# Deformable gather over 32 tiles of two image rows in place of 33 tiles of padded positions, with a table whose borders are zeroed once

## The chip, the cores and the metric

The kernel runs on one core of a Trainium2 chip. A core has a matrix engine (TensorE, PE in the profile, with PEld for its weight loads), a vector engine (VectorE, DVE), a scalar engine (ScalarE, ACT), a general engine (GpSimd, POOL) and a sync engine (SyncE, SP) that only issues transfers here. Data lie in SBUF, a memory of 128 partitions; matrix products accumulate in PSUM; DRAM holds inputs, outputs and scratch tables, and 16 DMA engines move data in and out. The metric is the device time in microseconds of one execution: 6844.52 us before the change, the median of three runs that lie between 6835.98 and 6856.77.

## What is computed

Four layers in sequence act on four images of 192 channels and 64 by 64 positions, all in float32. The change touches the first layer only, and of that the deformable convolution, which feeds a channel attention:

```python
def deform_conv(x, w_p, b_p, w_d):
    off = conv2d(x, w_p, stride=1, pad=1) + b_p      # 18 offsets a position
    xp = jnp.pad(x, ((0, 0), (0, 0), (1, 1), (1, 1)))
    Hp, Wp = (H + 2, W + 2)                          # 66 x 66
    ...
    px = off[:, :N] + p0x + pn[0]                    # N = 9 taps
    py = off[:, N:] + p0y + pn[1]
    ...
    xo = g_lt * gat(qlx, qly) + g_rb * gat(qrx, qry) \
       + g_lb * gat(qlx, qry) + g_rt * gat(qrx, qly)
    ...
    return conv2d(xo, w_d, stride=KS, pad=0)

xn = layer_norm(x)
q = deform_conv(xn, w_p, b_p, w_d)
k_spe, v_spe = qkv(xn)
attn = softmax(q @ l2norm(k_spe).T * temperature)
```

Every output position and each of its nine taps needs a blend of four neighbouring pixels, at places that are known only at run time. The products of `q` with `k_spe` are sums over positions, so the kernel never forms `q`: it sums the outer products of the blended pixels with the normed pixels over all positions, for every tap, and applies the weights afterwards.

## The kernel before, in words

**Geometry.** An image normed by the first layer is held in SBUF as `xn`, 2 halves of 96 channels on partitions, by 66 x 66 positions with a border of zeros (`WP` = 66). `MID` = 67 is the place of the first real pixel. The kernel cuts the stretch from `MID` on into `NT` = 33 tiles of 128 successive padded positions. Some positions of each tile are border columns, with pixels of zero, so that they add zero to the sums.

**The table.** For each image a table in DRAM has one row for each padded position, with four quarters of 192 floats: the pixel and its right, lower and lower-right neighbours (3072 bytes a row). One gathered row is all that one tap of one position needs. There are two tables, used in turn by image; they are zeroed at the head and tail once, when the kernel begins (lines 317 to 327).

**`offsets(b)`, line 404**, has four stages. Eight steps of layer norm load an eighth of the image each (`xi`, line 431) and write it into `xn`. `write_table` (line 455) turns each tile of 128 positions by two transposes on PE (line 462), copies it from PSUM into a buffer `tt` by ACT (line 463), and after a group of G tiles stores the buffer four times, once for each quarter, shifted by the neighbour's place (line 466): G is 11, so 3 groups and 12 stores, or 3 where it is woven between other work, so 11 groups and 44 stores. Then `xn` itself is stored for later (line 471). `convolve` (line 473) computes the 18 offsets of each position by matmuls of 96 x 32 weights and 384 columns (three tiles; line 482); four such column groups make a batch, so that 33 tiles are 11 groups in batches of 4, 4 and 3. The result is turned (line 490) and added to the base positions `p0` (line 494), an input of 128 x 33 x 18 floats that is loaded for every image. Eight operations on DVE (lines 503 to 515) make the row indices `idx` and the blend weights.

**`gather(b)`, line 518**, goes through the nine taps in five groups, `[(0, 1), (2, 3), (4, 5), (6, 7), (8,)]`, and in each over the 33 tiles. One tile of a group loads its own pixels from the table's last quarter (line 566, 96 KB; for the last group straight into half of `xo`), gathers the rows of each tap by an indirect transfer that POOL issues (line 572) into a ring of 11 buffers, blends them by two operations on ACT and two on DVE (lines 578 to 583), and multiplies: three matmuls of 128 x 128 by 192 columns (line 590), each of which is two PE instructions in float32. The buffers of the tile (`xo`, `ti`, `row`) are threefold.

**Order.** For image 0, `gather` runs alone from about 115 us to 624 us of the trace ("stage A"), with its pixels kept in SBUF (`kept`, 33 tiles), and `offsets(1)` is woven in between: one step of it every few steps of the gather. For images 1 to 3 the gather is woven into the non-local attention of layer 1 of the image before. That layer goes through 16 query chunks of 256 positions (scores at line 920, exponential at line 984, product with the values at line 986), and `GATHER_STEPS` = 33 x 9 + 12 tells the weaver over how many steps to spread the gather. For images 2 and 3, the layer-norm steps of `offsets` alternate with the key projection of layer 1 (line 865 on), and the rest of `offsets` runs right after it, before the first query chunk is loaded (`xc`, line 909) and its first matmul (`th`, line 912). I call these stretches, which end near 2515 us and 4135 us, the transitions.

SP issues all plain transfers in program order into one queue. In a transition that order is: table stores, store of `xn`, two loads of `xc`, three loads of `ti`, two more of `xc`, then weights.

Of the kernel before, what the change touches and what calls it, by code (L numbers as in the profile page):

```python
# [10 lines left out]
F32 = mybir.dt.float32  # L11
# [9 lines left out]
P = 96  # L21
# [21 lines left out]

TROWS = 35 * 128
RING = 11
GATHER_STEPS = NT * 9 + 12
TAPS = [(0, 1), (2, 3), (4, 5), (6, 7), (8,)]


# [30 lines left out]
def conv_seq_kernel(ctx: ExitStack, tc: tile.TileContext, a, out: bass.AP):  # L80
# [236 lines left out]
    with pool_of(name="zero", bufs=1) as zp:  # L317
        zero = zp.tile([128, 4 * C], F32, tag="zero", name="zero")
        nc.gpsimd.memset(zero, 0.0)
        for i in range(2):  # L320
            t = dram.tile([TROWS, 4 * C], F32, tag=f"table{i}", name=f"table{i}")
            first, last = 2 * WP + 2, WP + 1 + NT * 128
            nc.sync.dma_start(out=t[0:128], in_=zero)
            nc.sync.dma_start(out=t[128:first], in_=zero[: first - 128])
            nc.sync.dma_start(out=t[last : last + 128], in_=zero)
            nc.sync.dma_start(out=t[last + 128 : TROWS], in_=zero[: TROWS - last - 128])
            tables.append(t)

    xn_flat = [dram.tile([C, XNW], F32, tag=f"xnd{i}", name=f"xnd{i}") for i in range(2)]
# [75 lines left out]
    def offsets(b, pool, kept=None, woven=False):  # L405
# [3 lines left out]
        table = tables[b % len(tables)]  # L409


        pos = pool.tile([128, NT, 18], F32, name=f"pos_{b}", tag="pos")
        fr = pool.tile([128, NT, 18], F32, name=f"fr_{b}", tag="fr")
        idx = pool.tile([128, NT, 9], I32, name=f"idx_{b}", tag="idx")
        xn = big.tile([P, 2, XNW], F32, tag="x", name=f"xn_{b}")
        xnv = xn[:, :, 0 : WP * WP].rearrange("p k (r c) -> p k r c", r=WP)
        for k in range(2):
# [7 lines left out]
        with ExitStack() as s:  # L425
            sb = s.enter_context(pool_of(name="l0a", bufs=1 if woven else 2))
            s1 = s.enter_context(pool_of(name="l0a1", bufs=1))
            ps = s.enter_context(pool_of(name="l0aps", bufs=2, space=PSUM))
            for i in range(NCH):
                xi = sb.tile([P, 2, CN], F32, tag="xi", name=f"xi_{b}_{i}", bufs=2)  # L430
                nc.sync.dma_start(out=xi, in_=given(b)[:, :, bass.ts(i, CN)])
                layer_norm(
                    xi, CN, xnv[:, :, 1 + 8 * i : 9 + 8 * i, 1:65], sb, ps, f"l0_{b}_{i}",
                    affine=(V["l0_g1"], V["l0_b1"]), rows=8,
                )
                yield

            wp = s1.tile([P, 2, 9, 32], F32, tag="wp", name=f"wp_{b}")
            given_wp = s1.tile([P, 2, 9, 18], F32, tag="given_wp", name=f"given_wp_{b}")
            nc.sync.dma_start(out=given_wp, in_=a["wp"].rearrange("(k p) t o -> p k t o", p=P))  # L440
            nc.gpsimd.memset(wp, 0.0)
            nc.gpsimd.tensor_copy(wp[:, :, :, 0:18], given_wp)
            bp = s1.tile([128, 1], F32, tag="bp", name=f"bp_{b}")
            nc.gpsimd.memset(bp, 0.0)
            for q in range(4):
                nc.sync.dma_start(out=bp[32 * q : 32 * q + 18, :], in_=a["bp"])
            p0 = s1.tile([128, NT, 18], F32, tag="p0", name=f"p0_{b}")
            nc.sync.dma_start(out=p0, in_=a["p0"])

            G, T = 3 if woven else 11, 3  # L450

            def write_table():
                for g in range(NT // G):
                    if kept is None:
                        tt = sb.tile([128, G, C], F32, tag="tt", name=f"tt_{b}_{g}", bufs=3 if woven else 2)
                    else:
                        tt = kept[:, bass.ts(g, G)]
                    for j in range(G):
                        t0 = (g * G + j) * 128 + MID
                        pt = ps.tile([128, C], F32, tag="tr", name=f"pt_{b}_{g}_{j}")  # L460
                        for k in range(2):
                            nc.tensor.transpose(pt[:, bass.ts(k, P)], xn[:, k, t0 : t0 + 128], ident[:P, :P])
                        nc.scalar.copy(tt[:, j, :], pt)
                    for q in range(4):
                        e = g * G * 128 + (2 - q // 2) * WP + 2 - q % 2
                        nc.sync.dma_start(
                            out=table[e : e + G * 128, bass.ts(q, C)].rearrange("(j p) c -> p j c", p=128), in_=tt
                        )
                    if not woven or g % 3 == 2:
                        yield  # L470
                nc.sync.dma_start(out=xn_drams[b % 2], in_=xn)

            def convolve():
                for g0 in range(0, NT // T, 4):
                    ng = min(4, NT // T - g0)
                    m = 32 * ng
                    po = ps.tile([128, T * 128], F32, tag="off", name=f"po_{b}_{g0}", bufs=1)
                    for tap in range(9):
                        for k in range(2):
                            for q in range(ng):  # L480
                                o = (g0 + q) * T * 128 + (tap // 3) * WP + tap % 3
                                nc.tensor.matmul(  # L482
                                    po[32 * q : 32 * q + 32], lhsT=wp[:, k, tap, :], rhs=xn[:, k, o : o + T * 128],
                                    start=tap == 0 and k == 0, stop=tap == 8 and k == 1,
                                )
                    ot = sb.tile([128, T * 128], F32, tag="ot", name=f"ot_{b}_{g0}")
                    nc.scalar.activation(ot[:m], po[:m], AF.Identity, bias=bp[:m])
                    pp = ps.tile([128, T, 4, 32], F32, tag="tr", name=f"pp_{b}_{g0}")
                    for j in range(T):
                        nc.tensor.transpose(  # L490
                            pp[:, j, 0:ng, :].rearrange("p q o -> p (q o)"), ot[:m, bass.ts(j, 128)], ident[:m, :m]
                        )
                    tiles = slice(g0 * T, (g0 + ng) * T)
                    nc.vector.tensor_tensor(
                        pos[:, tiles, :].rearrange("p (q j) o -> p j q o", j=T), pp[:, :, 0:ng, 0:18],
                        p0[:, tiles, :].rearrange("p (q j) o -> p j q o", j=T), ALU.add,
                    )
                    yield

            for part in (convolve(), write_table()) if woven else (write_table(), convolve()):  # L500
                yield from part

            nc.vector.tensor_scalar(pos, pos, -1.0, 65.0, ALU.max, ALU.min)
            fi = s1.tile([128, NT, 18], I32, name=f"fi_{b}", tag="fi")
            fl = s1.tile([128, NT, 18], F32, name=f"fl_{b}", tag="fl")
            nc.vector.tensor_copy(fi, pos)
            nc.vector.tensor_copy(fl, fi)
            nc.vector.tensor_tensor(fr, fl, pos, ALU.is_gt)
            nc.vector.tensor_tensor(fl, fl, fr, ALU.subtract)
            nc.vector.tensor_tensor(fr, pos, fl, ALU.subtract)  # L510
            nc.vector.tensor_scalar(pos, fr, -1.0, 1.0, ALU.mult, ALU.add)
            nc.vector.scalar_tensor_tensor(
                fl[:, :, 0:9], fl[:, :, 0:9], float(WP), fl[:, :, 9:18], ALU.mult, ALU.add
            )
            nc.vector.tensor_scalar(idx, fl[:, :, 0:9], float(MID), None, ALU.add)
        return pos, fr, idx

    def gather(b, s, at, m2, kept=None):
# [16 lines left out]
        for taps in TAPS:  # L535
# [16 lines left out]
                nc.sync.dma_start(out=wd[64:128, 1:12:3, :], in_=a["wd"][0:64, 1:9:2, :])  # L552
                nc.sync.dma_start(out=wd[:, 2:12:3, :], in_=a["wd"][64:C, 1:9:2, :])
            acc = [ps.tile([128, 512], F32, tag=f"h{h}", name=f"h{h}_{b}_{taps[0]}") for h in range(2)]
            for t in range(NT):

                e = t * 128 + MID
                xo = sb.tile([128, 2, C], F32, tag="xo", name=f"xo_{b}_{t}_{taps[0]}")
                if kept is not None:
                    tt = kept[:, t]  # L560
# [2 lines left out]
                else:  # L563
                    tt = xo[:, 1, :]
                if kept is None:
                    nc.sync.dma_start(out=tt, in_=table[e : e + 128, 3 * C : 4 * C])
                elif len(taps) == 1:
                    nc.gpsimd.tensor_copy(xo[:, 1, :], tt)
                for j, tap in enumerate(taps):
# [18 lines left out]
                for m in range(3):  # L588

                    nc.tensor.matmul(  # L590
                        acc[m // 2][:, bass.ts(m % 2, C)], lhsT=xo.rearrange("p j c -> p (j c)")[:, bass.ts(m, 128)],
                        rhs=tt, start=t == 0 and m % 2 == 0, stop=t == NT - 1, skip_group_check=True,
                    )
                yield
            m = 3 * (taps[0] // 2)
# [1262 lines left out]
    with ExitStack() as s:  # L1858
        sb = s.enter_context(pool_of(name="l0first", bufs=1))
        m2 = stats.tile([M, C + 3 * M], F32, tag="m2", name="m2_0")  # L1860
        kept = sb.tile([128, NT, C], F32, tag="kept", name="kept")
        at = links(offsets(0, sb, kept))
        beside = [constants(), offsets(1, second, woven=True)]
        for k, _ in enumerate(gather(0, s, at, m2, kept)):
# [132 lines left out]
```

## Time and profile before

| what | value |
|---|---|
| median of three runs | 6844.52 us (6835.98 to 6856.77) |
| profiled execution, first to last instruction | 6951.6 us |
| its mean granted PE clock | 0.938 |
| PE busy | 6255.4 us (90%), 45188 instructions |
| DVE busy | 4817.8 us (69%) |
| ACT busy | 3725.4 us (54%) |
| POOL busy | 2061.6 us (30%) |
| DMA | 743.45 MB, mean 107 GB/s |
| gathers, line 572 | 1188 (4 images x 9 taps x 33 tiles) |
| matmul instructions of the gather, line 590 | 2376 + 990 + 594 |
| transposes, line 462 | 264 |
| offset convolution, line 482 | 1584 instructions |

The profiled execution took 107 us more than the median run, so a number from the trace is 1.6% larger than the same work in the runs that give the time. The page's busy times say how long an engine had an instruction in hand, not that it worked at its peak; a time on an engine costs something only where nothing else is later. In a table of windows, each row gives a stretch from the start of the span in microseconds, its length, the busy time of each engine with the instructions in brackets, the granted PE clock as a share of full speed, the mean busy share of the 16 DMA engines, and what they moved.

### The profile page before, as it was taken

How to read it: one execution, taken by the hardware profiler on the slowest of the kernel's cores; microseconds unless marked ns; L12 is line 12 of the kernel's file. 1: busy time of each engine (PE TensorE's matmuls, PEld its weight loads, DVE VectorE, ACT ScalarE, POOL GpSimd, SP SyncE). 2: the span in 40 equal slices, each digit the busy share in tenths (PEclk: the TensorE clock that was granted, in tenths of full speed). 3: DMA queues.
4: the chain of work that ended last, by engine and by line, in shares of the span. 5: the costliest groups of instructions: out<-in, count | busy, mean ns of one | idle time of the engine just before them, and what ended most of it. 6: DMA issues, size and time to landing. Idle time of an engine off the chain costs nothing.

```text
span 6951.6 us, 115213 instructions
## 1 busy us (share of the span) xinstructions
PE 6255.4 (90%) x45188; PEld 4235.5 (61%) x45188; DVE 4817.8 (69%) x7087; ACT 3725.4 (54%) x6214; POOL 2061.6 (30%) x2273
## 2 busy tenths in 40 slices
PE   7677999999988899999988899999998889999876
PEld 4445578886643468886654458887554457766432
DVE  3664279985577769985586849996576757765656
ACT  3664368874544358874544348885544325545331
POOL 2654057752200047761200017772210000012100
PEclk8888989999999999999989999999998979999988
DMA  7795257751010277762010067673110010010000
GB/s 229 257 317 180 70 161 225 226 180 36 21 28 13 62 237 227 220 214 57 11 42 12 21 216 217 220 222 102 32 29 22 14 52 10 14 36 12 7 3 20
DMA packets 362109, 743.45 MB, mean 107 GB/s; under 512 B 52647, under 2 KB 245335, under 8 KB 360798
## 3 DMA queue, kind: packets, MB, share of 16 engines
q0 software_dynamic: 95616, 469.38, 21.1%
q1 hardware_dynamic: 265950, 266.70, 12.9%
q8 instruction: 356, 5.83, 0.4%
q14 instruction: 187, 1.53, 0.1%
HBM read 628.06 MB, written 106.21 MB: 106 GB/s over the span
## 4 chain that ended last, share of the span: by engine, by line
PE 65%; DVE 17%; ACT 7%; issue 4%; DMA 4%; SPq 1%; another core or an unknown queue 1%; POOL 1%; DVEq 0%; ACTq 0%; POOLq 0%
PE s L920 11%; PE y L986 11%; PE h L590 7%; PE v L1151 2%; DVE ha L1328 2%; PE qk L1076 2%; PE h L1528 2%; DMA ring<-table,idx 2%; PE qk L1077 2%; DVE ga L1328 2%; PE po L482 2%; PE t L1159 1%; PE h L803 1%; DVE gate L1328 1%; PE zm L1539 1%
## 5 line engine op out<-in xcount | busy, mean ns | idle before, releaser
L572 POOL DMA_INDIRECT ring<-table,idx x1188 | 1657.7, 1395 | 1103.3 <-DVE row L579 273.2
L920 PE MATMUL s<-ths,ph 96*128 96x256 f32 x4096 | 981.6, 385 | 14.2 <-ACT ths L914 7.4
L920 PEld LDWEIGHTS s<-ths,ph 96*128 96x128 f32 x4096 | 782.8, 193 | 154.8 <-ACT ths L914 19.0
L578 ACT ACTIVATE row<-ring,pos 128x384 f32<-128x384 f32 x1188 | 697.7, 609 | 213.5 <-DVE xo L583 132.4
L579 DVE SCALAR_TENSOR_TENSOR row<-ring,fr,row 128x384 f32<-128x384 f32 x1188 | 696.9, 611 | 84.1 <-ACT row L578 56.8
L986 PE MATMUL y<-sc,gx 128*97 128x256 f32 x3008 | 720.1, 379 | 0.0
L582 ACT ACTIVATE xo<-row,pos 128x192 f32<-128x192 f32 x1188 | 504.6, 448 | 151.3 <-remote 73.1
L986 PEld LDWEIGHTS y<-sc,gx 128*97 128x97 f32 x3008 | 489.0, 164 | 125.7 <-issue 2.3
L583 DVE SCALAR_TENSOR_TENSOR xo<-row,fr,xo 128x192 f32<-128x192 f32 x1188 | 464.4, 411 | 106.9 <-ACT xo L582 59.6
L590 PE MATMUL h<-ti,xo 128*128 128x192 f32 x2376 | 460.3, 329 | 5.6 <-DVE xo L583 5.6
L922 ACT COPY sc<-s 128x1024 f32<-128x1024 f32 x376 | 377.3, 1003 | 164.1 <-PE s L920 155.1
L983 DVE TENSOR_TENSOR sc<-sc,mbs 128x1024 f32<-128x1024 f32 x376 | 446.7, 1216 | 20.9 <-ACT mbs L946 13.7
L927 DVE TENSOR_TENSOR top<-top,sc 128x1024 f32<-128x1024 f32 x282 | 344.5, 1222 | 149.5 <-ACT sc L922 133.9
L590 PEld LDWEIGHTS h<-ti,xo 128*128 128x128 f32 x2376 | 404.4, 191 | 40.4 <-DVE xo L583 11.7
L984 ACT ACTIVATE sc<-sc 128x1024 f32<-128x1024 f32 x376 | 392.5, 1053 | 39.2 <-DVE sc L983 36.6
L1135 DVE TENSOR_REDUCE es<-ex 128x6 f32<-128x384 f32 x264 | 133.3, 546 | 358.8 <-ACT ex L1131 358.8
L590 PE MATMUL h<-kept,xo 128*128 128x192 f32 x990 | 261.9, 402 | 121.4 <-DVE xo L583 61.7
L1569 POOL COPY gate<-gate 128x192 f32<-128x192 f32 x12 | 4.2, 351 | 1115.2 <-ACT gate L1562 1115.2
L590 PEld LDWEIGHTS h<-kept,xo 128*128 128x128 f32 x990 | 191.2, 226 | 203.6 <-DVE xo L583 92.9
L1328 DVE SCALAR_TENSOR_TENSOR ga<-gate,v,ga 128x1024 f32<-128x1024 f32 x234 | 299.7, 1281 | 7.2
L986 PE MATMUL y<-se,gx 128*97 128x256 f32 x1088 | 260.4, 379 | 0.5 <-ACT yn L992 0.5
L1533 ACT ACTIVATE z<-h,bias_fc1T 128x512 f32<-128x512 f32 x192 | 118.0, 687 | 230.2 <-PE h L1530 229.9
(390 smaller groups left out, 11548.6 us busy)
## 6 DMA issues: line engine op xcount, KB each, us to landing
ti<-table SPq DMA_DIRECT2D x396, 96.0 KB
table<-tt SPq DMA_DIRECT2D x24, 1056.0 KB
ring<-table,idx POOLq DMA_INDIRECT x1188
xnd<-xn SPq DMA_DIRECT2D x4, 3270.0 KB
table<-kept SPq DMA_DIRECT2D x12, 1056.0 KB
table<-tt SPq DMA_DIRECT2D x44, 288.0 KB
xi<-in_x_dram SPq DMA_DIRECT2D x32, 384.0 KB
xk<-xd SPq DMA_DIRECT2D x32, 384.0 KB
```

Of the source, the lines that this page charges most:

```text
L572: nc.gpsimd.indirect_dma_start(out=gt.rearrange("p r q c -> p (r q c)"), out_offset=None, in_=table[:, :], in_offset=bass.IndirectOffsetOn ...
L578: nc.scalar.activation(row, gt[:, :, 0, :], AF.Copy, scale=pos[:, t, 9 + tap : 10 + tap])
L579: nc.vector.scalar_tensor_tensor(row, gt[:, :, 1, :], fr[:, t, 9 + tap : 10 + tap], row, ALU.mult, ALU.add)
L582: nc.scalar.activation(xo[:, j, :], row[:, 0, :], AF.Copy, scale=pos[:, t, tap : tap + 1])
L583: nc.vector.scalar_tensor_tensor(xo[:, j, :], row[:, 1, :], fr[:, t, tap : tap + 1], xo[:, j, :], ALU.mult, ALU.add)
L590: nc.tensor.matmul(acc[m // 2][:, bass.ts(m % 2, C)], lhsT=xo.rearrange("p j c -> p (j c)")[:, bass.ts(m, 128)], rhs=tt, start=t == 0 and ...
L920: nc.tensor.matmul(p[:, t, :], lhsT=ph[:, bass.ts(G * g + t, 128)], rhs=ths[i], start=True, stop=True)
L922: nc.scalar.copy(to, p)
L983: nc.vector.tensor_tensor(ex, ex, mbs[i].unsqueeze(1).to_broadcast([128, G, QN]), ALU.add)
L984: nc.scalar.activation(ex, ex, AF.Exp)
L986: nc.tensor.matmul(py, lhsT=gx[:, G * g + t, :], rhs=ex[:, t, :], start=g == 0 and t == 0, stop=g == NG - 1 and t == G - 1,)
L1328: nc.vector.scalar_tensor_tensor(acc[:, b], src(tap, b), w[:, tap : tap + 1], acc[:, b], ALU.mult, ALU.add)
```

## The change

Tiles become two image rows of 64 real pixels: tile t holds rows 2t and 2t + 1, with the first row on partitions 0 to 63 and the second on 64 to 127. There are then 32 tiles, a tile begins every 2 x 66 table rows, and border columns are in no tile. Since no tile writes the border columns of the table any more, these are zeroed at the beginning, by one transfer for each quarter and table, and the tail of zeros begins later. The transposes become four matmuls with the identity for each tile, one for each image row and half of the channels. Each store of the table and each load of the tile's own pixels becomes two, one for each half of the partitions, since the two halves lie 66 table rows apart. G becomes 8 (4 groups, 32 stores), or 4 where woven (8 groups, 64 stores), and the buffer `tt` is twofold in both. The offset convolution works on four tiles (512 columns) at a time, in two batches of four column groups, and reads its columns as eight stretches of 64. The base positions are built from three small loads and ten operations on POOL instead of one load of 128 x 33 x 18 floats.

```diff
-GATHER_STEPS = NT * 9 + 12
+NU, UT = 32, 2 * WP
+GATHER_STEPS = NU * 9 + 12
...
-            first, last = 2 * WP + 2, WP + 1 + NT * 128
+            first, last = 2 * WP + 2, MID + NU * UT - 2
...
+            for q in range(4):
+                e = (2 - q // 2) * WP + 2 - q % 2 + W
+                pads = t[e : e + (H - 1) * WP].rearrange("(i w) c -> i w c", w=WP)[:, 0:2, bass.ts(q, C)]
+                nc.sync.dma_start(out=pads, in_=zero[0 : H - 1, 0 : 2 * C].rearrange("p (w c) -> p w c", w=2))
...
-            p0 = s1.tile([128, NT, 18], F32, tag="p0", name=f"p0_{b}")
-            nc.sync.dma_start(out=p0, in_=a["p0"])
-
-            G, T = 3 if woven else 11, 3
+            p0 = s1.tile([128, NU, 18], F32, tag="p0", name=f"p0_{b}")
+            for to, of, t in (((0, W), (0, W), 0), ((W, 2 * W - 2), (WP, 2 * W), 0), ((2 * W - 2, 2 * W), (0, 2), 1)):
+                nc.sync.dma_start(out=p0[slice(*to), 0, :], in_=a["p0"][slice(*of), t, :])
+            n = 1
+            while n < NU:
+                nc.gpsimd.tensor_scalar_add(p0[:, n : 2 * n, 0:9], p0[:, 0:n, 0:9], 2.0 * n)
+                nc.gpsimd.tensor_copy(p0[:, n : 2 * n, 9:18], p0[:, 0:n, 9:18])
+                n *= 2
+
+            G, T = 4 if woven else 8, 4
...
-                        tt = sb.tile([128, G, C], F32, tag="tt", name=f"tt_{b}_{g}", bufs=3 if woven else 2)
+                        tt = sb.tile([128, G, C], F32, tag="tt", name=f"tt_{b}_{g}", bufs=2)
...
-                            nc.tensor.transpose(pt[:, bass.ts(k, P)], xn[:, k, t0 : t0 + 128], ident[:P, :P])
+                            for h in range(2):
+                                nc.tensor.matmul(
+                                    pt[bass.ts(h, W), bass.ts(k, P)], lhsT=xnv[:, k, r0 + h, 1 : W + 1], rhs=ident[:P, :P],
+                                    start=True, stop=True,
+                                )
...
-                        e = g * G * 128 + (2 - q // 2) * WP + 2 - q % 2
-                        nc.sync.dma_start(
-                            out=table[e : e + G * 128, bass.ts(q, C)].rearrange("(j p) c -> p j c", p=128), in_=tt
-                        )
-                    if not woven or g % 3 == 2:
+                        e = g * G * UT + (2 - q // 2) * WP + 2 - q % 2
+                        to = table[e : e + G * UT, bass.ts(q, C)].rearrange("(j r w) c -> r w j c", r=2, w=WP)
+                        for h in range(2):
+                            nc.sync.dma_start(out=to[h, 0:W], in_=tt[bass.ts(h, W)])
+                    if not woven or g % 2 == 1:
...
-                for g0 in range(0, NT // T, 4):
-                    ng = min(4, NT // T - g0)
-                    m = 32 * ng
+                for g0 in range(0, NU // T, 4):
+                    ng, m = 4, 128
...
-                                    po[32 * q : 32 * q + 32], lhsT=wp[:, k, tap, :], rhs=xn[:, k, o : o + T * 128],
+                                    po[32 * q : 32 * q + 32].rearrange("p (r c) -> p r c", c=W), lhsT=wp[:, k, tap, :],
+                                    rhs=xnv[:, k, r0 : r0 + 2 * T, c0 : c0 + W],
...
-            for t in range(NT):
-
-                e = t * 128 + MID
+            for t in range(NU):
+
+                e = t * UT + MID
...
-                    nc.sync.dma_start(out=tt, in_=table[e : e + 128, 3 * C : 4 * C])
+                    for h in range(2):
+                        at0 = e + WP * h
+                        nc.sync.dma_start(out=tt[bass.ts(h, W)], in_=table[at0 : at0 + W, 3 * C : 4 * C])
...
-        kept = sb.tile([128, NT, C], F32, tag="kept", name="kept")
+        kept = sb.tile([128, NU, C], F32, tag="kept", name="kept")
```

## The prediction, made before the changed kernel was run

> **What bounds the kernel now.** I read the chain of waits first (the work that ended last, followed back, as shares of the span), then the rows of instruction groups that the change touches, then windows over the three places where the change works.
>
> ```profile
> PE 65%; DVE 17%; ACT 7%; issue 4%; DMA 4%; SPq 1%; another core or an unknown queue 1%; POOL 1%; DVEq 0%; ACTq 0%; POOLq 0%
> L572 POOL DMA_INDIRECT ring<-table,idx x1188 | 1657.7, 1395 | 1103.3 <-DVE row L579 273.2
> L590 PE MATMUL h<-ti,xo 128*128 128x192 f32 x2376 | 460.3, 329 | 5.6 <-DVE xo L583 5.6
> ti<-table SPq DMA_DIRECT2D x396, 96.0 KB
> table<-tt SPq DMA_DIRECT2D x24, 1056.0 KB
> ```
>
> PE sets most of the end; POOL's gathers alone are no bound (its share is 1%). The L590 row says that one more busy instruction of the gather costs PE 460.3/2376 = 0.194 us at the granted clock of this run (they overlap, so busy over count and not the 329 ns of one); read start to start at full clock it is 0.162. The last two rows are the transfers that will be cut in two.
>
> ```profile
> 448.00:527.00 79.00, 48.12 (x193) 36.47 (x192) 44.54 (x97) 46.33 (x120) 46.54 (x45) 0.78 1.04 387
> 860.00:1610.00 750.00, 733.53 (x3567) 605.14 (x3565) 622.88 (x1005) 551.23 (x930) 450.44 (x301) 0.97 0.61 189
> 2515.00:3220.00 705.00, 687.83 (x3395) 574.93 (x3394) 617.47 (x997) 545.04 (x921) 457.52 (x304) 0.99 0.64 200
> 2485.00:2495.00 10.00, 9.98 (x122) 3.79 (x114) 0.00 (x0) 0.00 (x0) 0.00 (x0) 1.00 1.09 371
> ```
>
> Columns after the length: PE, PEld, DVE, ACT, POOL busy, granted clock, DMA share, GB/s. Three regimes are to be seen. In stage A (first row: the stretch in which image 1's table is stored beside image 0's gathers) PE has slack and the DMA engines are full at 387 GB/s. With a gather inside layer 1 (rows two and three) PE is 98% busy and DMA is at 0.61 to 0.64. At the end of a transition (last row) both are full.
>
> **The change part by part** (sums against the 6951.6 us span; the median is 0.985 of it).
>
> *Nine gathers fewer in stage A.* The first gather is issued at 114.9, the last of 297 at 623.9: 1.72 us each, in every part of the stage. Nine by 1.72 is 15.5 us. The lower bound is what DMA alone gives back: a gather brings 128 x 3072 B = 0.39 MB, nine 3.5 MB, at 387 GB/s 9.1 us. I take **-13**, as the woven work between is not shorter.
>
> *One tile fewer in each layer-1 stage.* Its work on PE is 15 matmuls, 30 instructions, by 0.162 us at a clock of 0.99: 4.9 us; PE is the bound there, so three images give **-14.6**. POOL, DVE and ACT lose nine taps too, off the bound.
>
> *Twice as many loads of a tile's pixels.* SP issues 160 more per image at 0.32 to 0.40 us each; SP has hardly anything else to do in a stage of 700 us. In the first four tap groups the loads run ahead. In the last, the load goes into half of `xo` and is issued only when that buffer is free; the waits of PE show how close it is already:
>
> ```profile
> PE h L590 <- DMA xo<-table: 1.5, 2, 0.8
> ```
>
> (image 1; 0.9 and 0.8 in the others). The second half is issued some 0.37 us after the first and each half reaches fewer partitions. If every tile were late by 0.37, it would be 32 by 0.37 = 12 us for an image, but a tile comes only every 2.1 us and has three buffers. Bounds 0 and +14 for three images; I take **+4**, near the row above.
>
> *Convolution, two full batches.* Four column groups run together: a round took 0.3235 us for 384 columns, 108 rounds are 34.9 us. After it, 72 rounds of 512 columns, by 512/384 of that, are 31.1: -3.9 us. Reading columns in stretches of 64 costs nothing by the nearest rows: matmuls of 512 columns with strided rows of 66 (line 722) and without (line 825) both take 430 ns.
>
> *Transposes by matmul.* Before:
>
> ```profile
> L462 PE MATMUL pt<-ident,xn 96*128 96x96 f32 x264 | 44.7, 283 | 18.9 <-ACT tt L463 13.2 <-issue 3.9 <-ACT xn L385 1.0
> 1701.09 0.89 PE L1151 MATMUL v<-qkvT,xw 96*64 96x96 f32 x16
> ```
>
> Two instructions, some 0.23 us, for each of 33 tiles. After: four matmuls of two instructions with 64-column weights. The second row (a timeline entry: 16 instructions in 0.89 us) is just that form; it runs in pairs, 0.08 us a pair in the middle, so 0.32 us for a tile: 10.2 against 7.6 us, +2.6. With the convolution PE gets about -1.3 in each `offsets`.
>
> *Table stores by halves.* This is the disputed term. In a transition the queue goes: 12 stores, `xn`, `xc`, and what ends it is not PE's own work:
>
> ```profile
> 2459.00:2482.00 23.00, 22.40 (x223) 10.96 (x216) 9.14 (x11) 12.15 (x29) 0.00 (x0) 1.00 1.09 369
> 2495.00:2505.00 10.00, 9.33 (x87) 3.77 (x90) 0.38 (x1) 0.58 (x1) 0.00 (x0) 1.00 1.06 366
> 2505.00:2511.00 6.00, 3.43 (x33) 1.16 (x26) 1.68 (x4) 0.58 (x1) 0.00 (x0) 0.92 0.78 215
> PE th L912 <- DMA xc<-xd: 2.2, 1, 2.2
> ```
>
> DMA is full from 2459 to 2505, PE is done at about 2508, and `xc` lands at 2511.4, 2.2 us after PE would want it (2.0 in image 3). So PE's own -1.3 is hidden, and each microsecond of longer stores is paid. A store set is 12.6 MB after (13.0 before); 128-partition stores of 1056 KB go at 370 GB/s, so 34 us. For stores from 64 partitions the trace has one row, the output stores of line 1793, two halves in succession at the very end:
>
> ```profile
> 6947.90:6950.00 2.10, 0.00 (x0) 0.00 (x0) 0.00 (x0) 0.00 (x0) 0.00 (x0) 0.50 0.95 250
> 6948.00:6949.10 1.10, 0.00 (x0) 0.00 (x0) 0.00 (x0) 0.00 (x0) 0.00 (x0) 0.50 0.99 199
> 6949.20:6950.00 0.80, 0.00 (x0) 0.00 (x0) 0.00 (x0) 0.00 (x0) 0.00 (x0) 0.50 0.96 338
> ```
>
> The pair goes at 205 to 250 GB/s, the first half alone at 199, the second at 338, with the engines full throughout. The Trainium skill speaks against the change here: by "SBUF — State Buffer", section "Door 1: The DMA port swizzle (why [64,N] ≈ [32,N])", 64 partitions reach half of the ports and get 196 GB/s where 128 get 328, and two transfers on the two halves gain only 6%. By that rule the set takes 12.6 MB / 196 GB/s = 64 us; by the pair's row, 50 to 61; by the 128-partition rows, 34. The row agrees with the rule in its first half only. As eight stores of each half follow each other in the queue, I expect the two to overlap, and take about 267 GB/s, 47 us, +13 of transfer. Groups of 8 tiles let the first store start near 2454 instead of 2457.5, `xn` and `xc` are unchanged, and 2.2 us of the wait can't be saved twice: **+4 per transition, +8**; bounds -3 and +17 each. In the front of image 0 the same stores stand before `xn`; the table landed about 7 us before `idx`, which releases the first gather: -1 from PE, bounds -1 to +6. In stage A image 1's stores are 12.6 MB within a full DMA mix: **+4**, bounds 0 and +19 (the same 13 us, plus the loss of the third `tt` buffer, on whose stores ACT waits already).
>
> *At no price:* eight border stores (126 pieces of 768 B each) and the zeros at the beginning, hidden by the layer norm of image 0, which is not done before 72 us; without that cover, about 1 us. The ten POOL operations and three small loads for `p0` run beside the layer norm's tail while POOL is idle in the transitions; the first of them is needed only by line 494, tens of microseconds later. In stage A they stand in POOL's queue before gathers, behind three small loads: some 2 us at worst. Eight DVE operations get 3% shorter: 0.1 us on the path to `idx`.
>
> **Sum:** -13 - 14.6 - 1 + 4 + 8 + 4 = -12.6 us of 6951.6, so 6939; times 0.985 it is **6832**, I say **6831**. A difference of 0.3% (20.5 us) is about what a measurement of this kernel can tell from no change.
>
> **Rivals.**
>
> *Halves cost nothing.* Stores and loads by halves run as wide ones do, since the next half is always queued behind. For it: the second half's 338 GB/s, and that packets of 768 B keep the engines full either way. Against: the first half's 199. Then -15.5 - 14.6 - 1 - 3 - 3 = -37 us, **6808**.
>
> *The port limit decides (slower).* One mechanism: a store from 64 partitions goes at the pair's 217 GB/s or below, in all sets. Place: the table stores before `xc` and in stage A's full DMA. Price: 58 us against 34; `xc` late by 14 in each transition (+28), stage A +19, the front +5, loads of `xo` +7. With -13 - 14.6 it is +31, **6875**. It decides from where the stores' rate falls below about 245 GB/s: there a set is 51 us, 4 more than I took, paid in two transitions and in stage A, and the 12.6 us of gain are gone. For it: the first half's row and the rule. Against: the second half's row.
>
> *The two halves wait for each other.* If each half's store waited for the one before to land, 32 stores by some 2 us of landing would add 40 us or more to each set, **6950** or above. Against: the two halves of line 1793 are issued without such a wait.
>
> **How the numbers follow.** Chances: forecast 0.38, halves free 0.31, port limit 0.26, waiting halves 0.05. The forecast's own range is 6818 to 6850, of which a small part is beyond 0.3%. Faster: 0.31 + 0.05 = 0.36; same: 0.34 (with a little from the port limit's mild end); slower: 0.30. The range reaches to the free case with its bounds, **6798**, and past the port limit to **6885**; below it lies little and above it the waiting halves.
>
> **What would show it.** In the changed trace: DMA GB/s and share while `table<-tt` is stored in the transitions (270 right; 360 the free case; 215 the port limit); the wait of L912 for `xc<-xd` (6 us right, 16 the port limit); first to last gather in stage A (496 us right); layer-1 stages about 4 us shorter from the first gather to the last; L590 waiting for `xo<-table` (a few us); 1152 instructions of the convolution with 512 columns, 0.43 us a round; the transposes at about 0.32 us a tile. The forecast is wrong if the stores leave 245 to 330 GB/s, or if PE's saving in layer 1 goes into another wait.

## The result, and the profile after

The changed kernel takes 6865.34 us, the median of 20 runs (6833.61 to 6898.30), where the kernel before takes 6838.12 us in 20 runs beside it (6807.31 to 6860.26). The ratio is 1.0046, with a 95% interval of 1.0029 to 1.0063: it is slower, by about 31 us (the two medians differ by 27). The time lies inside the range of the prediction, but on the other side of no change than the predicted time, close to the rival that let the stores of half the partitions decide (6875).

Before anything is read from the two profiles, one thing has to be put right. The profiled execution of before (span 6951.6) and that of after (6896.5) were taken, to judge by their stages, on different chips: on one the kernel before takes about 6840 us, on another about 6950, with 508 us in stage A as in the first profile. Stage by stage the two can't be compared. The 107 us by which the first profile was longer than the median run are also not spread evenly, as I took them to be: 49 of them lie in stage A. I therefore took the kernel before again on a chip where it takes 6835 us (span 6825.5), and all differences below are against that profile, unless I say otherwise.

The page of after, rows of the groups and of the DMA issues that answer to those shown before:

```profile
PE 67%; DVE 16%; ACT 7%; DMA 5%; issue 3%; SPq 1%; POOL 0%; POOLq 0%; ACTq 0%; DVEq 0%
L589 POOL DMA_INDIRECT ring<-table,idx x1152 | 1645.1, 1428 | 1046.6 <-DMA xc<-xd 289.8
L607 PE MATMUL h<-ti,xo 128*128 128x192 f32 x2304 | 449.5, 329 | 22.0 <-DMA ti<-table 15.7
ti<-table SPq DMA_DIRECT2D x768, 48.0 KB
table<-tt SPq DMA_DIRECT2D x64, 384.0 KB
```

The tiles are gone as meant: 1152 gathers for 1188, 2304 matmul instructions for 2376. Two rows carry bad news. The largest part of POOL's idle time before a gather (289.8 of 1046.6 us) is now put down to `xc<-xd`, the load that ends a transition. And PE, which before was idle 5.6 us ahead of the gather's matmuls, is idle 22.0 us, most of it for `ti<-table`.

The windows show where the time went. They are from a second profile of the changed kernel, on a chip of the same kind as the new profile of before; the first to the last gather of stage A, and then the three layer-1 stages with a gather woven in, before (first fence) and after (second):

```profile
111.30:571.40 460.10, 344.86 (x1721) 226.56 (x1722) 306.57 (x641) 303.87 (x663) 320.32 (x335) 0.83 0.90 307
836.70:1528.80 692.10, 684.95 (x3398) 574.03 (x3397) 616.29 (x997) 544.71 (x921) 447.65 (x293) 0.99 0.61 195
2434.70:3129.20 694.50, 686.23 (x3396) 574.01 (x3396) 619.37 (x1002) 544.52 (x921) 462.80 (x304) 0.99 0.65 204
4040.00:4736.50 696.50, 688.67 (x3396) 575.48 (x3396) 619.47 (x1002) 544.59 (x921) 461.13 (x303) 0.99 0.64 203
```

```profile
113.90:556.70 442.80, 343.14 (x1772) 224.06 (x1772) 297.24 (x621) 296.12 (x643) 315.96 (x325) 0.84 0.92 311
823.50:1508.60 685.10, 678.15 (x3368) 567.24 (x3367) 608.37 (x979) 537.29 (x903) 440.65 (x284) 1.00 0.62 191
2436.70:3139.20 702.50, 685.95 (x3366) 572.24 (x3366) 608.25 (x978) 537.72 (x903) 450.73 (x295) 0.98 0.64 196
4064.60:4762.20 697.60, 682.21 (x3366) 569.84 (x3366) 608.21 (x978) 537.24 (x903) 456.64 (x294) 0.99 0.64 198
```

The second column is the length of the stage. With the transitions (from the first matmul `tp` of the key projection to the first `th`, line 929) the ledger is:

| stage, us | before | changed, 1st profile | changed, 2nd profile |
|---|---|---|---|
| up to the first gather | 111.3 | 117.9 | 113.9 |
| stage A, first to last gather | 460.1 | 447.5 | 442.8 |
| layer 1, gather of image 1 within | 692.1 | 684.6 | 685.1 |
| transition, offsets of image 2 | 107.6 | 135.4 | 134.5 |
| layer 1, gather of image 2 within | 694.5 | 697.0 | 702.5 |
| transition, offsets of image 3 | 107.9 | 135.0 | 134.3 |
| layer 1, gather of image 3 within | 696.5 | 701.6 | 697.6 |

Stage A gains 13 to 17 us, each transition loses 27, and of the gain in layer 1 only the first stage keeps anything. These rows add up to +49 and +41 us. That is more than the 31 us of the 20 runs, but the stretches between the rows, whose code the change does not touch, differ by up to 22 us each from one profile to the next.

Now a transition itself. SP's queue as the timeline has it (start, length, issues), before and then after:

```profile
2380.85 33.41 SPq L466 DMA_DIRECT2D table<-tt  x12
2414.30 3.67 SPq L471 DMA_DIRECT2D xnd<-xn  x1
2418.07 3.14 SPq L909 DMA_DIRECT2D xc<-xd  x2
```

```profile
2358.33 60.09 SPq L483 DMA_DIRECT2D table<-tt  x32
2418.46 1.47 SPq L486 DMA_DIRECT2D xnd<-xn  x1
2420.03 3.76 SPq L926 DMA_DIRECT2D xc<-xd  x2
```

The stores are issued over 60.1 us, not 33.4; what follows in the queue is unchanged, and so `xc` is late. PE's wait for it in this transition:

```profile
PE th L929 <- DMA xc<-xd: 22.0, 1, 22.0
```

Windows over the stores show two causes. Before (first fence), and after:

```profile
2380.80:2400.80 20.00, 20.00 (x210) 9.77 (x203) 7.85 (x9) 10.71 (x27) 0.00 (x0) 1.00 1.05 346
2407.20:2419.00 11.80, 11.11 (x135) 4.28 (x135) 0.38 (x1) 0.59 (x2) 0.00 (x0) 1.00 1.01 342
```

```profile
2358.30:2380.80 22.50, 22.50 (x224) 10.98 (x228) 8.95 (x11) 10.07 (x21) 0.00 (x0) 1.00 0.88 244
2380.90:2386.40 5.50, 5.50 (x70) 2.56 (x64) 0.00 (x0) 1.77 (x7) 0.00 (x0) 1.00 0.51 155
2397.00:2407.50 10.50, 10.50 (x108) 4.02 (x102) 0.00 (x0) 1.77 (x6) 0.00 (x0) 1.00 0.25 69
2407.60:2420.00 12.40, 6.31 (x46) 1.98 (x42) 5.46 (x11) 0.73 (x2) 0.00 (x0) 0.85 0.84 229
```

**Rate:** while stores run, they go at 229 to 244 GB/s, not 342 to 346. A packet of 768 B takes 43.8 ns (the mean of the 15964 packets in this stretch) in place of 36.1, which for 16 busy engines is 281 in place of 340 GB/s, and the engines are no longer full (0.84 and 0.88). **Gaps:** twice the stores stop (rows of 155 and 69 GB/s), since the next group of eight tiles isn't in its buffer. PE's timeline over the second gap shows what stands in its way:

```profile
2391.53 11.35 PE L496 MATMUL po<-xn,wp 96*32 96x512 f32 x98 [0.78 <-ACT ot L502]
2402.80 0.88 PE L474 MATMUL pt<-ident,xn 96*64 96x96 f32 x16
```

The transposes of the last group (line 474) come behind 98 instructions of the convolution, 11.35 us, in PE's order. With two buffers, the fourth group can't be turned until the stores of the second have landed.

The rate belongs to this place, not to half stores as such. In stage A, where the stores of image 1 share the DMA engines with the gathers of image 0, the windows over them are alike, whole (first line, before) and halved (second line, after):

```profile
406.00:468.00 62.00, 36.21 (x163) 28.14 (x161) 36.27 (x78) 38.50 (x104) 33.99 (x33) 0.78 1.04 378
412.00:500.00 88.00, 63.86 (x388) 47.17 (x387) 53.14 (x119) 56.36 (x143) 58.88 (x56) 0.78 1.02 381
```

The engines are full in both, and a packet of 768 B takes 36.1 ns before and 36.3 after. Why halves are slow only where they have the engines almost to themselves, no run here shows.

### The profile page after: what moved, and what is told of

It is laid out like the page before. It is cut to its first block, busy times and chain, and to the rows that moved or that the text cites. A ratio compares the mean times of both kernels' runs of the same rounds, so it can differ in the third digit from the quotient of the medians.

```text
span 6896.5 us, 116257 instructions
## 1 busy us (share of the span) xinstructions
PE 6226.2 (90%) x45392; PEld 4204.3 (61%) x45392; DVE 4783.7 (69%) x7011; ACT 3702.5 (54%) x6134; POOL 2075.5 (30%) x2276
## 4 chain that ended last, share of the span: by engine, by line
PE 67%; DVE 16%; ACT 7%; DMA 5%; issue 3%; SPq 1%; POOL 0%; POOLq 0%; ACTq 0%; DVEq 0%
PE s L937 13%; PE y L1003 11%; PE h L607 7%; PE v L1168 2%; DMA ring<-table,idx 2%; PE po L496 2%; PE qk L1093 2%; DVE ha L1345 2%; PE h L1545 2%; DVE ga L1345 2%; PE qk L1094 2%; PE t L1176 1%; PE h L820 1%; DVE gate L1345 1%; PE zm L1556 1%
## 5 line engine op out<-in xcount | busy, mean ns | idle before, releaser
L589 POOL DMA_INDIRECT ring<-table,idx x1152 | 1645.1, 1428 | 1046.6 <-DMA xc<-xd 289.8
L595 ACT ACTIVATE row<-ring,pos 128x384 f32<-128x384 f32 x1152 | 675.6, 610 | 244.5 <-DVE xo L600 156.6
L596 DVE SCALAR_TENSOR_TENSOR row<-ring,fr,row 128x384 f32<-128x384 f32 x1152 | 675.7, 613 | 114.8 <-ACT row L595 108.9
L599 ACT ACTIVATE xo<-row,pos 128x192 f32<-128x192 f32 x1152 | 488.8, 448 | 73.3 <-DVE row L596 37.8
L600 DVE SCALAR_TENSOR_TENSOR xo<-row,fr,xo 128x192 f32<-128x192 f32 x1152 | 450.2, 412 | 40.1 <-ACT xo L599 38.2
L607 PE MATMUL h<-kept,xo 128*128 128x192 f32 x960 | 247.6, 392 | 75.3 <-DVE xo L600 68.6
L607 PEld LDWEIGHTS h<-kept,xo 128*128 128x128 f32 x960 | 176.0, 217 | 165.2 <-DVE xo L600 127.6
```

The source lines that it names most:

```text
L589: nc.gpsimd.indirect_dma_start(out=gt.rearrange("p r q c -> p (r q c)"), out_offset=None, in_=table[:, :], in_offset=bass.IndirectOffsetOn ...
L595: nc.scalar.activation(row, gt[:, :, 0, :], AF.Copy, scale=pos[:, t, 9 + tap : 10 + tap])
L596: nc.vector.scalar_tensor_tensor(row, gt[:, :, 1, :], fr[:, t, 9 + tap : 10 + tap], row, ALU.mult, ALU.add)
L599: nc.scalar.activation(xo[:, j, :], row[:, 0, :], AF.Copy, scale=pos[:, t, tap : tap + 1])
L600: nc.vector.scalar_tensor_tensor(xo[:, j, :], row[:, 1, :], fr[:, t, tap : tap + 1], xo[:, j, :], ALU.mult, ALU.add)
L607: nc.tensor.matmul(acc[m // 2][:, bass.ts(m % 2, C)], lhsT=xo.rearrange("p j c -> p (j c)")[:, bass.ts(m, 128)], rhs=tt, start=t == 0 and ...
```

## The experiments

My theory (A) was: the loss is in the transitions, by the rate of half stores and by the gaps on top. Its rivals were that the rate alone sets the end, that halves are nearly free and the gaps are all, and that the loss is not the stores but the doubled loads of the gather. The first four kernels ran on a chip where the kernel before takes 6949.83 us (30 runs).

**The kernel before, for a second profile** (unchanged).

> The kernel before, for a second profile. Theory A (the first profile's stage A of 509 us from the first to the last gather is an unusually slow execution) expects 440 to 480 us there and about 24 us less than the changed kernel in each transition (first LN chunk of image 2 to the first matmul of its first query chunk). The rival, that stage A of this kernel is always that slow, expects 500 us or more again.

Stage A took 507.9 us, so my reading of the first profile as an unusual execution was wrong; on this chip the stage takes so long in this kernel, and 506.7 in the one with halved stores below. The transitions took 107.8 us each, as on the other.

**The changed kernel on that chip.**

> The changed kernel on the same chip as the others: ratio 1.003 to 1.006, with PE waiting about 22 us for xc<-xd in each transition of images 2 and 3. If that wait was an accident of one profile, it is below 10 us here.

The ratio is 1.0126 (1.0097 to 1.0156), a larger loss than expected. The transitions take 135.2 and 135.8 us, the waits for `xc` are there (21.7 us for image 2). But on this chip stage A gains only 7.5 us (500.4), and the layer-1 stages too are 7 to 18 us longer than before. There ACT and DVE wait at places for which the profile shows no releaser ("remote" and "issue"); on the other chip the changed kernel's stage has almost no such waits. What these are was not settled.

**Four buffers for `tt`**, so that no group waits for a store:

```diff
-tt = sb.tile([128, G, C], F32, tag="tt", name=f"tt_{b}_{g}", bufs=2)
+tt = sb.tile([128, G, C], F32, tag="tt", name=f"tt_{b}_{g}", bufs=2 if woven else 4)
```

> The changed kernel with a fourfold table buffer tt in the offsets that are not woven. Theory A (half-partition stores are slower, and on top the last group of eight tiles comes too late: with two buffers its transposes stand behind 11 us of convolution in PE's order, so that the store queue runs dry for some 15 us) expects the wait for xc<-xd to fall from 22 to about 6 us in both transitions, 32 us less in all, and a ratio of 0.998 to 1.002. The rival (the rate of half stores alone sets the end, the gaps only fill what it leaves) expects at most 5 us per transition, a wait of 17 us or more and a ratio of 1.003 or above.

The ratio is 1.0061 (1.0031 to 1.0091) beside 1.0126 for the changed kernel. The transitions took 125.7 and 121.9 us: 10 and 14 less, not the 16 I expected, and the wait is 15.5 us in image 2, neither side's number. Gaps are part of it, and not the larger part.

**The kernel before with its table stores halved**, the rest of the source kept:

```diff
+to = table[e : e + G * 128, bass.ts(q, C)].rearrange("(j p) c -> p j c", p=128)
+for h in range(2):
+    nc.sync.dma_start(out=to[64 * h : 64 * h + 64], in_=tt[64 * h : 64 * h + 64])
```

> The kernel before with every table store cut into two of 64 partitions, all else kept. If the rate of half stores is the main loss (packets of 768 B in 44 ns, not 36): the stores of a transition take 8 to 13 us longer, xc is late by as much, stage A 5 to 15 us longer: ratio 1.003 to 1.006. If halves are nearly free and the loss comes from groups of eight tiles with two buffers: ratio 0.999 to 1.001 and a wait for xc of below 6 us.

The ratio is 1.0027 (1.0009 to 1.0045), a little under the band; stage A did not grow. In the transitions the halves cost more than I expected: 127.2 and 123.6 us against 107.8. The stores take 49.9 us, and the wait that was 2 us is 16.4 (timeline of SP and wait of PE of this kernel):

```profile
2470.66 49.89 SPq L468 DMA_DIRECT2D table<-tt  x24
PE th L912 <- DMA xc<-xd: 16.4, 1, 16.4
```

So cutting the stores in two makes 16 to 19 us of a transition in the kernel before. It isn't their rate alone: in this kernel too the stores stop before the last group, as its transposes now stand behind 98 instructions of the convolution (8.57 us; in the kernel before the two alternate):

```profile
2471.00:2496.00 25.00, 24.02 (x254) 11.33 (x254) 9.14 (x11) 11.70 (x26) 0.00 (x0) 1.00 1.00 311
2500.00:2508.00 8.00, 8.00 (x79) 3.30 (x74) 0.38 (x1) 2.48 (x9) 0.00 (x0) 1.00 0.02 6
2508.00:2521.00 13.00, 12.31 (x115) 4.62 (x111) 0.38 (x1) 0.58 (x1) 0.00 (x0) 1.00 0.92 267
```

The next four ran where the kernel before takes 6835.09 us (33 runs).

**The kernel before once more**, the profile that the ledger above uses.

> The kernel before once more, for the ledger of stages on the chip of the next three runs; no theory expects a change. If this chip is one on which this kernel takes about 6840 us and not 6950, stage A is about 450 us instead of 508, and the stalls of ACT in stage A that the page puts down to 'remote' (64 us before) are gone.

Stage A took 460.1 us here, and the stalls of ACT are gone with the 48 us.

**A tile fewer, and nothing else:** the kernel before with 32 of its 33 gather tiles (the last tile's positions are left out of the sums).

```diff
-for t in range(NT):
+for t in range(NT - 1):
```

> The kernel before with a gather over its first 32 tiles only (the last tile's positions, about two image rows, are left out of the sums), all else kept: what nine gathers and 15 matmuls fewer for each image are worth by themselves. The prediction's terms say -13 in stage A and -14.6 in layer 1: ratio 0.996, between 0.9945 and 0.9975. If the gain is not there at all (the gather is hidden, or waits take its place), 0.999 to 1.001.

The ratio is 0.993 (0.9907 to 0.9952). The profile has stage A at 448.9 us (-11.2) and the layer-1 stages at 688.4, 691.0 and 691.1 (-3.7, -3.5, -5.4): together -24, near the -27.6 of the prediction. The rest of the ratio is in stretches that the edit doesn't touch, and six runs are few. The gain of the tiles is real.

**A hybrid:** gather, convolution and image 0 as changed, but the tables of images 1 to 3 turned and stored by 33 tiles of 128 positions, as before. The stores write the border columns as zeros.

```diff
 def write_table():
+    if kept is None:
+        G = 3 if woven else 11
+        for g in range(NT // G):
...
+        return
+    G = 8
```

> The changed kernel, but the tables of images 1 to 3 are transposed and stored as before (33 tiles of 128 positions, stores of 128 partitions); gather, loads by halves, convolution and image 0 as changed. Theory A (the loss is the stores: rate plus gaps) expects the transitions back at 108 us from tp to th, -27 each against the changed kernel, and the gain of the tiles to show: ratio 0.995 to 0.999. The rival (the layer-1 stages lose by the doubled loads of ti and xo) expects transitions as before but layer 1 longer by 5 to 15 us a stage than before: ratio 1.000 to 1.005.

The ratio is 0.9984 (0.9967 to 1.0001), within A's band. The transitions are 110.4 and 110.0 us; with wide stores 24 to 25 of the 27 us are back. The layer-1 stages, 682.9, 693.5 and 700.3, don't gain in image 3: PE waits for a `ti` load there, 7.3 us, as in the changed kernel.

**The kernel before with the loads of `ti` and `xo` halved.**

```diff
-nc.sync.dma_start(out=tt, in_=table[e : e + 128, 3 * C : 4 * C])
+for h in range(2):
+    nc.sync.dma_start(out=tt[64 * h : 64 * h + 64], in_=table[e + 64 * h : e + 64 * h + 64, 3 * C : 4 * C])
```

> The kernel before with each load of a tile's own pixels (ti, xo) cut into two of 64 partitions, all else kept. The prediction's term for it is +4 us, ratio 1.0006, at most +14 or 1.002. The rival, that the doubled loads are what makes layer 1 of the changed kernel longer, expects 5 to 15 us more in each of three stages: ratio 1.002 to 1.007.

The ratio is 0.9997 (0.9979 to 1.0015): doubled loads cost nothing here, and PE waits for `xo` 0.9 to 1.4 us a stage, where it was 0.6 to 0.9. That rival falls, for the tiles of the kernel before.

The last four ran beside 75 runs of the kernel before (6835.68 us).

**The changed kernel as their neighbour.**

> The changed kernel again, as the neighbour of the next three: ratio 1.003 to 1.007 on a chip where the kernel before takes about 6840 us, 1.010 to 1.015 where it takes about 6950 us.

1.0058 (1.0039 to 1.0077), as expected.

**Four buffers for `tt`, again.**

> The changed kernel with the fourfold table buffer, again, beside the changed kernel. If the gaps in the stores cost 10 to 14 us per transition (as the first run of it showed, tp to th 122 to 126 us against 135), the ratio to the changed kernel is 0.995 to 0.998. If that run's gain was scatter and only the rate of half stores counts, 0.999 to 1.001.

The ratio to before is 1.0025 (1.0007 to 1.0043); against its neighbour that is 1.0025/1.0058 = 0.9967, within the band. Timeline of SP, wait of PE, and a window over the whole of the stores of image 2:

```profile
2378.40 50.80 SPq L483 DMA_DIRECT2D table<-tt  x32
PE th L929 <- DMA xc<-xd: 15.2, 1, 15.2
2379.00:2429.00 50.00, 49.20 (x506) 21.28 (x506) 8.78 (x12) 14.55 (x34) 0.00 (x0) 1.00 0.91 240
```

No store waits for its buffer now. What remains is the rate: stores over 50.8 us and a wait of 15.2 in image 2, 47.3 and 11.7 in image 3. The transitions, 126.8 and 124.0 us, put the gaps at 8 to 10 us each, and what half stores leave at 16 to 19. No run stores whole partitions in such small pieces in a transition (384 KB each, where the kernel before has 1056), so the halves and the size of a store are not told apart there.

**The hybrid with four buffers for `ti`** (`bufs=4` where the pool gives three). PE's order is the same as in the hybrid.

> The hybrid (wide stores for images 1 to 3, all else as changed) with four buffers for ti in place of three; PE's order of instructions is the same. In the hybrid PE waits 7 us for ti<-table at the beginning of layer 1 of image 3, at a low granted clock after it. If that load is late because its buffer is freed late, the wait falls below 2 us in each stage and layer 1 gets 5 to 10 us shorter for images 2 and 3: ratio 0.995 to 0.998. If it is late because the queues are full at that moment, the wait stays at 5 us or more, and the ratio is that of the hybrid, 0.997 to 1.000.

The ratio is 0.9978 (0.9961 to 0.9996). PE's longest waits in layer 1 with the gather of image 3, in the hybrid with three buffers (first fence) and with four (second):

```profile
PE h L624 <- DMA ti<-table: 7.3, 1, 7.3
PE th L946 <- DMA xc<-xd: 6.9, 1, 6.9
```

```profile
PE th L946 <- DMA xc<-xd: 6.9, 1, 6.9
PE mb L978 <- DVE dg L975: 2.4, 7, 1.0
PE h L624 <- DVE xo L617: 2.1, 2, 1.7
```

The wait for `ti` is gone from the list, and the stage takes 692.1 us, 8.2 less than in the hybrid and 4.4 less than before. In the hybrid, then, the load was late because its buffer came free late. The ratio can't tell this kernel from the hybrid.

**The same with three buffers for `tt`** in images 2 and 3.

> The same with three buffers for tt in the offsets that are not woven, so that no group of 11 tiles waits for a store to land (a gap of 6 us in the stores of the kernel before). If gaps matter for wide stores as for half ones, xc lands 3 to 6 us earlier in each transition, as far as PE's own end (2 us before) lets it count: 0.994 to 0.997. If PE's own end takes over, the same as hybrid_ti4 within 0.0005.

The ratio is 0.9977 (0.9963 to 0.9991), the same as without, as the second reading has it; but not for its reason. The gaps between the three groups stay (6.0 and 4.9 us), and so does the wait for `xc` (6.8 us): with wide stores it is not the buffer that a group waits for. This hybrid and the one above it are the two complete versions that are faster than both kernels beyond their interval, by 0.2%.

## Why the prediction was wrong, step by step

The sum was -12.6 us; the rows of the two profiles give +49 and +41. Of this miss of 54 to 62 us, the transitions make 45 to 47 and layer 1 makes 11 to 13.

**Nine gathers fewer in stage A, -13, and its table stores by halves, +4:** the gathers are right. The stage measured -12.6 and -17.3 in the two profiles, -11.2 with the tile alone left out. The price of the stores isn't there: their packets take no longer in this stage, and the three hybrids, which store whole there, aren't faster (448.4 to 454.1 us; 442.8 and 447.5 in the changed kernel).

**Front, -1:** measured +6.6 and +2.6, but the kernel before itself takes 111.3 to 114.9 us to its first gather, so that no price is shown.

**One tile fewer in layer 1, -14.6, and its loads by halves, +4:** right as a price for the tile (-12.6 for the tile alone), but the changed kernel keeps it only in the first stage (-7). In the other two it ends at +1 to +8, by a wait that I had not priced: some 30 us into the stage PE stands still for one `ti` load, 9.2 us in image 2 and 7.6 in image 3 of the second profile, and for 24 and 14 us from shortly before that its granted clock is 0.50, where in the kernel before it is so for 3 and 7 us. This window is around the wait in image 3:

```profile
4087.00:4107.00 20.00, 10.61 (x39) 8.24 (x40) 11.88 (x21) 8.44 (x14) 12.27 (x8) 0.66 0.82 254
```

I had looked for the price of halved loads in the last tap group (`xo`, +4). There the wait stayed at about 1 us. A fourth buffer for `ti` takes the wait away in the hybrid; in the changed kernel itself that was not run. With four `tt` buffers the changed kernel stops at the same place for the blended `xo` instead (6.9 and 5.6 us; in image 2 DVE has 4.5 us of the scores' multiplications ahead of the blend), and its second and third stage, 696.5 and 698.1 us, gain nothing either.

**Convolution -3.9, transposes +2.6:** the first is right. From the last layer-norm write to the end of the convolution, PE takes 28.6 us before and 23.6 in the hybrid, which has the new convolution and the old transposes. The second was mis-sized: with the new transposes it is 34.1 us. Some of that is transposes that now come after that write instead of ahead of it; the rest is that they alternate with the convolution, and four of its instructions take 1.05 us between transposes where they take 0.46 in a long run (11.35/98 by 4): two of them begin together there, and four in the long run. PE's own end is not on the path, as PE waits 22 us after it; the last group's transposes are, through the stores that wait for them.

**Table stores by halves, +4 per transition with bounds of -3 and +17:** this is the step that failed; it measured +27 (and so +54 in the sum, where +8 stood). The transfer was near the mark where nothing interrupts it: I took 267 GB/s and 47 us for a set, and with four buffers a set took 47 to 51 us (248 to 266 GB/s). From this I had 13 us of longer transfer. Then I let an earlier start, 3.5 us, and the slack of the chain take most of it back, and neither happened: the first store is issued 56 us after the transition begins, 54 before. What half stores leave without gaps is 16 to 19 us. And I priced a store set as one stretch of transfer, without asking whether the next group would be in its buffer: two buffers of eight tiles, with the last group's transposes behind the convolution, left the queue idle for 10 us more, and 8 to 10 us of the transition come back with four buffers. This split of the 27 rests on that one edit, run twice; the halved stores of the kernel before also cost 16 to 19, but with a stop of their own. Both bounds were built from transfer alone, which is why even the upper one was too low.

The trace of before had a sign of this. I wrote that DMA is full from 2459 to 2505; the windows shown leave out the three microseconds in which it is not, while SP waits 6.1 us for the last group to be in its buffer:

```profile
2482.00:2485.00 3.00, 3.00 (x33) 1.46 (x37) 0.38 (x1) 0.86 (x3) 0.00 (x0) 1.00 0.57 194
```

Both signs that I had named for a wrong forecast came: while stores run they leave the band of 245 to 330 GB/s (229 to 244), and PE's saving in layer 1 goes into another wait.

**The rule against the row:** by "SBUF — State Buffer" of the Trainium skill ("Door 1": 196 GB/s) I had estimated 64 us for a set. Stores of one half and then the other, queued behind each other, took 47 to 51 us without gaps, 12.6 MB at 248 to 266 GB/s: in a transition halves are dear, but less than by the rule, and in stage A they are not dear at all. The gain of only 6% for two transfers on the two halves stands on that page under "Can I just issue two DMAs to hit both halves?". The sign that the rule pointed to was right for the transitions.

**The rivals:** "halves cost nothing" falls in the transitions and holds in stage A. "The port limit decides" had the sign and nearly the time, but by luck: it had +28 for the two transitions and +19 for stage A, and the profiles show +53 to +55 and no price. Its rate of 217 GB/s is not what was measured, and what it missed in the transitions is mostly the gaps, which it did not have.

## What to carry to other kernels

A layout that saves work may cut every transfer into halves of the partitions: price that by the time of one packet in each stretch (36 against 44 ns in the transitions here, 36 and 36 beside the gathers), above all where a load stands behind the stores in the queue. Then ask whether the stores are fed: buffers times group size, and what is ahead of the next group in the producer's order. And where the reader's layout gains and the writer's loses, try them apart: the hybrid keeps the one without the other.

## What was not expected of the hardware

PE's granted clock differs between executions in a stretch of the same code. The key projection of the last image, with nothing woven in, took 29 us in the new profile of before and 51 us in the first profile of after:

```profile
5535.00:5564.00 29.00, 27.79 (x160) 19.35 (x159) 3.90 (x7) 5.46 (x8) 0.00 (x0) 1.00 0.44 115
```

```profile
5582.00:5633.00 51.00, 49.65 (x161) 33.75 (x159) 3.90 (x7) 5.47 (x8) 0.00 (x0) 0.56 0.25 66
```

The clock was 1.00 in one and 0.56 in the other. It belongs to neither kernel: the first profile of before has 51.6 us there, the second of after 28.8. A single such stretch is two thirds of the effect measured here, so that one profile of each kernel can't settle it. And chips differ: the same kernel takes 6835 or 6950 us, and the change costs 0.5% on the one and 1.3% on the other.
